# Sigmoids ahead of the gating steps, more buffers and one shift for four tiles, in the first stage of a triangle kernel

## The chip, the cores and the metric

The kernel runs on one core of a Trainium2 chip. The metric is the time of one execution on the device, in microseconds (us). The program is one launch; all five engines (TensorE, VectorE, ScalarE, GpSimd, SyncE) and the DMA work in it side by side. In the profile PE is TensorE's matmuls, PEld its weight loads, DVE is VectorE, ACT is ScalarE, POOL is GpSimd and SP is SyncE, which here only issues transfers.

## The reference

Two layers on `x` of 384 x 384 positions with 128 channels, all in float32. The first is a triangle product, the second a gated row operation. Cut to what matters:

```python
def layer0(x, ...):
    z = layernorm(x)                                   # over the channels
    left = (z @ Wl + bl) * sigmoid(z @ Wlg + blg)
    right = (z @ Wr + br) * sigmoid(z @ Wrg + brg)
    core = einsum('bikh,bjkh->bijh', left, right)
    zo = layernorm(core) @ Wout + bout
    return x + sigmoid(x @ Wg + bg) * zo

def layer1(pair, ...):
    left = pair @ (W_left + W_eq) + b_left + b_eq
    right_sum = sum(pair @ W_right + b_right, axis=2)
    out = left * right_sum * sigmoid(pair @ W_gate + b_gate)
    return layernorm(out @ W_out + b_out + pair)
```

## The kernel before

It has three stages. The first makes `left` and `right` of all positions and writes them to the scratch tensor `lr_d`; it also writes the transposed, normalized input to `xt_d` for the third. The second makes `core`, one channel `h` at a time. The third does the rest. The change lies in the first and at the seam to the second.

The first stage works in chunks of eight rows `i` by 128 positions `k` (144 chunks), each in two steps of four tiles of 128 positions by 128 channels: 288 steps. Sixteen steps fill one `lr` tile of 64 rows (a block; there are 18), which is then stored in eight slices. Pools and the parts of a step (line numbers as the profile has them, cuts marked with `...`):

```python
inp = ctx2.enter_context(tc.tile_pool(name="p2in", bufs=3))           # lrh, second stage
...
with tc.tile_pool(name="p1x", bufs=6, side="right") as xp, \
     tc.tile_pool(name="p1w", bufs=2, side="right") as wp, \
     tc.tile_pool(name="p1s", bufs=5, side="right") as sp, \
     tc.tile_pool(name="p1z", bufs=4, side="right") as ztp, \
     ...
     tc.tile_pool(name="p1t", bufs=2, space=PSUM) as tps, \
     tc.tile_pool(name="p1p", bufs=3, space=PSUM) as pps:

    def stats(n, q, half):                    # L223, L225, VectorE: two bn_stats, two bn_aggr
        ...
    def powers(n, q):                         # L236 to L239, GpSimd: rs, and nd = mean - std of eight tiles
        ...
    def shift(n, q):                          # L248, GpSimd
        kb, ig, c = chunks[n]
        z = wp.tile([P, 4, C], F32, tag="z", name="z")
        for r in range(4):
            rr = 4 * q + r
            nd = nds[kb, ig][:, c * XR + rr:c * XR + rr + 1]
            seq(nc.gpsimd.tensor_scalar(z[:, r, :], loaded[n][:, rr, :], nd, None, ALU.subtract))
        return z

    def front(n, q, z):                       # L255 TensorE, L257 ScalarE
        pt = tps.tile([P, 4, P], F32, tag="pt", name="pt")
        for r in range(4):
            seq(nc.tensor.transpose(pt[:, r, :], z[:, r, :], ident))
        zt = zts[n, q] = ztp.tile([P, 4, P], F32, tag="zt", name="zt")
        seq(nc.scalar.copy(zt, pt))

    def store_zt(n, q):                       # L262, SP
        ...
        seq(nc.sync.dma_start(out=xt_d[:, i0:i0 + 4, kb, :], in_=zts.pop((n, q))))

    def store_slice():                        # L276, SP: one eighth of a full lr tile to lr_d
        ...

    def back(n, q, half):                     # L291 TensorE, L298 ScalarE, L299 VectorE
        ...
        t = lr[kb, ig]
        pr = pps.tile([P, 2, 4 * H], F32, tag="pr", name="pr")
        for r in range(2):
            seq(nc.tensor.matmul(pr[:, r, :], lhsT=zts[n, q][:, 2 * half + r, :], rhs=wz, start=True, stop=True))
        sg = wp.tile([P, 2, 2 * H], F32, tag="sg", name="sg")
        for r in range(2):
            rr = 4 * q + 2 * half + r
            rs = normed[n][2][:, rr:rr + 1]
            seq(nc.scalar.activation(sg[:, r], pr[:, r, 2 * H:], AF.Sigmoid, scale=rs))
            seq(nc.vector.scalar_tensor_tensor(
                t[:, :, c * XR + rr, :],
                pr[:, r, :2 * H].rearrange("k (h s) -> k h s", s=2),
                rs,
                sg[:, r].rearrange("k (h s) -> k h s", s=2),
                ALU.mult, ALU.mult,
            ))
        ...

    for k, (n, q) in enumerate(steps):
        if k + 2 < len(steps):
            zs[k + 2] = shift(*steps[k + 2])
        if k + AHEAD - 1 < len(steps):        # AHEAD = 6
            powers(*steps[k + AHEAD - 1])
        for half in range(2):
            back(n, q, half)
            if half == 0 and k + 1 < len(steps):
                front(*steps[k + 1], zs.pop(k + 1))
            if k + AHEAD < len(steps):
                stats(*steps[k + AHEAD], half)
        if q == NQ - 1:
            del loaded[n], normed[n]
            load_chunk(n + 6)                 # L114, SP
            if chunks[n][2] == G // XR - 1:
                store_nd(*chunks[n][:2])      # a small transpose and store at the end of a block
        store_zt(n, q)
        store_slice()
        ...
        if k == 20:
            late_weights()                    # L197 to L212: weights of the later stages
        if k == len(steps) - 2 * G // 4 + 16:
            for h in range(3):
                load_h(h)                     # L92, L93, SP: lrh tiles of the first three channels
```

So one step on TensorE is two matmuls of 128x512, four transposes for the next step, and two matmuls more; in float32 each matmul shows in the profile as two records. Pools hand out their tiles in turn: a tile can be written again when its last reader is done, be it an engine or a transfer. The scheduler keeps each engine's instructions in program order. In the second stage, nine matmuls a channel read an `lrh` tile and an `rr` tile filled from it; when a channel is done, the tile of the channel three later is loaded.

Of the kernel before, what the change touches and what calls it, by code (L numbers as in the profile page):

```python
# [8 lines left out]
F32 = mybir.dt.float32  # L9
AF = mybir.ActivationFunctionType  # L10
ALU = mybir.AluOpType
# [3 lines left out]
P = 128  # L15
# [4 lines left out]
def triangle_then_gated_row_kernel(ctx: ExitStack, tc: tile.TileContext, a: dict, out: bass.AP):  # L20
# [12 lines left out]
    nc = tc.nc  # L33
    x = a["x"].rearrange("b i j c -> (b i) j c")
    y = out.rearrange("b i j c -> (b i) j c")
    N, _, C = x.shape
    H = a["L0_conv_Wl"].shape[1]
    assert C == P and H == P and N % P == 0
    NB = N // P
    G = 64  # L40
    NG = N // G
    XR = 8
# [13 lines left out]
    def seq(ins):  # L56

        return tc.keep_in_program_order(ins)
# [20 lines left out]
    end2 = ctx.enter_context(ExitStack())  # L79
    with ExitStack() as ctx2:  # L80
        lrp = ctx2.enter_context(tc.tile_pool(name="lr", bufs=2))
        inp = ctx2.enter_context(tc.tile_pool(name="p2in", bufs=3))
        loaded2 = {}

        def load_h(h):

            if h < H:
                t = inp.tile([P, NB, N, 2], F32, tag="lrh", name="lrh")
                src = lr_d[h].rearrange("(b p) i s -> p b (i s)", p=P)
                i1 = 2 * G * (NG - KEEP)  # L90
                dst = t.rearrange("p b i s -> p b (i s)")
                seq(nc.sync.dma_start(out=dst[:, :NB - 1], in_=src[:, :NB - 1]))  # L92
                seq(nc.sync.dma_start(out=dst[:, NB - 1, :i1], in_=src[:, NB - 1, :i1]))  # L93
                loaded2[h] = t

        with tc.tile_pool(name="p1x", bufs=6, side="right") as xp, \
             tc.tile_pool(name="p1w", bufs=2, side="right") as wp, \
             tc.tile_pool(name="p1s", bufs=5, side="right") as sp, \
             tc.tile_pool(name="p1z", bufs=4, side="right") as ztp, \
             tc.tile_pool(name="p1d", bufs=2, side="right") as dp, \  # L100
             tc.tile_pool(name="p1t", bufs=2, space=PSUM) as tps, \
             tc.tile_pool(name="p1p", bufs=3, space=PSUM) as pps:
# [3 lines left out]
            loaded, normed = {}, {}  # L106
# [83 lines left out]
            def late_weights():  # L190

                ps = tps.tile([P, 4, P], F32, tag="pt", name="pw")
                m2 = wp.tile([P, 4, C], F32, tag="z", name="m2")[:, 0]
                seq(nc.vector.tensor_scalar(m2, avg, go, -1.0, ALU.mult, ALU.mult))
                seq(nc.tensor.matmul(ps[:, 0], lhsT=m2, rhs=wout0, start=True, stop=True))  # L197
                seq(nc.vector.scalar_tensor_tensor(wc, wout0, go, ps[:, 0], ALU.mult, ALU.add))
                seq(nc.tensor.matmul(ps[:, 1, 0:1], lhsT=wout0, rhs=bo, start=True, stop=True))
                seq(nc.vector.tensor_add(bz, ps[:, 1, 0:1], bout0))  # L200

                seq(nc.vector.tensor_add(wleft, wleft, weq))
                seq(nc.vector.tensor_add(bleft, bleft, beq))
                for n, (w, b) in enumerate(((wleft, bleft), (wgate, bgate), (wright, bright))):
                    p4 = ps[:, 2, n:n + 1]
                    seq(nc.tensor.matmul(p4, lhsT=w, rhs=bout1, start=True, stop=True))
                    seq(nc.vector.tensor_sub(b, b, p4))
                seq(nc.vector.tensor_scalar(bright, bright, float(N), None, ALU.mult))  # L210

                seq(nc.vector.tensor_scalar(lns, lns, -1.0, None, ALU.mult))  # L212
# [14 lines left out]
            def powers(n, q):  # L227


                if q == NQ - 1:  # L230
                    _, mv, rs, sd = normed[n]
                    kb, ig, c = chunks[n]
                    if c == 0:
                        nds[kb, ig] = dp.tile([P, G], F32, tag="nd", name="nd")
                    nd = nds[kb, ig][:, c * XR:(c + 1) * XR]
                    seq(nc.gpsimd.tensor_scalar(sd, mv[:, :, 1], EPS, 1.0, ALU.add, ALU.mult))  # L236
                    seq(nc.gpsimd.tensor_tensor(rs, sd, mhalf[:, :XR], ALU.pow))
                    seq(nc.gpsimd.tensor_tensor(sd, sd, rs, ALU.mult))
                    seq(nc.gpsimd.tensor_tensor(nd, mv[:, :, 0], sd, ALU.subtract))  # L239

            def shift(n, q):

                kb, ig, c = chunks[n]
                z = wp.tile([P, 4, C], F32, tag="z", name="z")
                for r in range(4):
                    rr = 4 * q + r
                    nd = nds[kb, ig][:, c * XR + rr:c * XR + rr + 1]
                    seq(nc.gpsimd.tensor_scalar(z[:, r, :], loaded[n][:, rr, :], nd, None, ALU.subtract))  # L248
                return z

            def front(n, q, z):
# [6 lines that stand above are left out]
# [24 lines left out]
            def back(n, q, half):  # L282


                kb, ig, c = chunks[n]
                if c == 0 and q == 0 and half == 0:
                    lr[kb, ig] = lrp.tile([P, H, G, 2], F32, tag="lr", name="lr")
# [3 lines that stand above are left out]
                    seq(nc.tensor.matmul(  # L291
                        pr[:, r, :], lhsT=zts[n, q][:, 2 * half + r, :], rhs=wz, start=True, stop=True
                    ))
                sg = wp.tile([P, 2, 2 * H], F32, tag="sg", name="sg")
                for r in range(2):
                    rr = 4 * q + 2 * half + r
                    rs = normed[n][2][:, rr:rr + 1]
                    seq(nc.scalar.activation(sg[:, r], pr[:, r, 2 * H:], AF.Sigmoid, scale=rs))  # L298
                    seq(nc.vector.scalar_tensor_tensor(  # L299
                        t[:, :, c * XR + rr, :],  # L300
                        pr[:, r, :2 * H].rearrange("k (h s) -> k h s", s=2),
                        rs,
                        sg[:, r].rearrange("k (h s) -> k h s", s=2),
                        ALU.mult, ALU.mult,
                    ))
                if c == G // XR - 1 and q == NQ - 1 and half == 1:
                    if (kb, ig) in kept:
                        kept[kb, ig] = t
                    else:
                        full.extend((kb, ig, hs, t) for hs in range(0, H, HS))  # L310
# [3 lines left out]
            nds, zts = {}, {}  # L314
# [12 lines left out]
# [3 lines that stand above are left out]
                if k + AHEAD - 1 < len(steps):  # L330
# [9 lines that stand above are left out]
                    load_chunk(n + 6)  # L340
                    if chunks[n][2] == G // XR - 1:
                        store_nd(*chunks[n][:2])
                store_zt(n, q)
                store_slice()
                if k == 4:
                    for t, src in later:
                        load(t, src)
                if k == 20:
                    late_weights()
                if k == len(steps) - 2 * G // 4 + 16:  # L350
                    assert not full
                    for h in range(3):
                        load_h(h)


        rrp, spool, rp = (end2.enter_context(tc.tile_pool(name=n, bufs=b, side="right", reuse_waits="tile"))
                     for n, b in (("p2r", 2), ("stats", 1), ("rstd", 2)))
        with tc.tile_pool(name="p2out", bufs=2, side="right", reuse_waits="tile") as op, \
             tc.tile_pool(name="p2sq", bufs=1, side="right", reuse_waits="tile") as qp, \
             tc.tile_pool(name="p2ps", bufs=2, space=PSUM, reuse_waits="tile") as ps:  # L360
            csum = spool.tile([P, NB, N], F32, name="csum")
# [1 line left out]
            seq(nc.vector.memset(csum, 0.0))  # L363
            seq(nc.vector.memset(csq, 0.0))

            right = {}

            def fill(h):
# [13 lines left out]
            for h in range(H):  # L382
                fill(h + 1)
                t, rr = loaded2.pop(h), right.pop(h)
# [23 lines left out]
    with ExitStack() as ctx3:  # L408
# [3 lines left out]
        xp, fp, inp, op = pool("p3x", 7), pool("p3f", A + 4), pool("p3in", 3), pool("p3out", 3)  # L412
        wp, sp, late = pool("p3w", 4), pool("p3s", 4), []
# [275 lines left out]
```

## Time and profile before

| | |
|---|---|
| time, median of 3 (lowest, highest) | 3457.69 us (3457.24, 3458.84) |
| span of the profiled execution | 3460.0 us |
| TensorE matmuls busy | 3363.2 us, 97% |
| VectorE, ScalarE, GpSimd busy | 2528.3, 2014.3, 2627.0 us |
| first stage, first projection to first matmul of the second | 15.4 to 1273.2 us |
| second stage | 1273.2 to 2016.0 us |
| third stage | 2016.0 to 3460.0 us |
| DMA, first stage | 229 GB/s |
| `zt` store: issue to landing, median | 5.4 us |
| `lr_d` slice store, chunk load | 7.1, 6.8 us |

The profile is one execution on the chip. A group is all instructions of one line, engine and operation; its row gives the tile written and those read, shapes, count, busy time, mean duration in ns, and then the idle time of that engine just before them with what ended most of it. A timeline row has start, length, engine, line, operation and count, and in brackets the idle time before and who ended it. The ends of matmuls are modelled, since they are pipelined: a busy TensorE need not be at its full pace, and the starts of records tell more than their lengths. Idle time of an engine that isn't on the path that sets the end costs nothing.

### The profile page before, as it was taken

How to read it: one execution, taken by the hardware profiler on the slowest of the kernel's cores; microseconds unless marked ns; L12 is line 12 of the kernel's file. 1: busy time of each engine (PE TensorE's matmuls, PEld its weight loads, DVE VectorE, ACT ScalarE, POOL GpSimd, SP SyncE). 2: the span in 40 equal slices, each digit the busy share in tenths (PEclk: the TensorE clock that was granted, in tenths of full speed). 3: DMA queues.
4: the chain of work that ended last, by engine and by line, in shares of the span. 5: the costliest groups of instructions: out<-in, count | busy, mean ns of one | idle time of the engine just before them, and what ended most of it. 6: DMA issues, size and time to landing. Idle time of an engine off the chain costs nothing.

```text
span 3460.0 us, 48243 instructions
## 1 busy us (share of the span) xinstructions
PE 3363.2 (97%) x12584; PEld 1986.6 (57%) x12584; DVE 2528.3 (73%) x8074; ACT 2014.3 (58%) x4049; POOL 2627.0 (76%) x4131
## 2 busy tenths in 40 slices
PE   8999999999999999999999989999999999999997
PEld 3444444444444446666666656777777777777775
DVE  6676677667766755555555568888888888888887
ACT  4555555555555543333333356777777777777776
POOL 7788788778877865656555538888888888888887
PEclk9999999999999999999999999999999999999999
DMA  5888778887888749999999987888888999888883
GB/s 141 231 256 257 224 227 255 250 241 220 255 252 245 215 150 282 281 282 285 281 284 282 282 285 230 265 272 272 273 271 272 273 274 274 271 271 270 271 269 101
DMA packets 924616, 872.90 MB, mean 252 GB/s; under 512 B 24868, under 2 KB 839720, under 8 KB 924344
## 3 DMA queue, kind: packets, MB, share of 16 engines
q1 hardware_dynamic: 904960, 794.32, 73.6%
q0 software_dynamic: 13152, 71.37, 10.1%
q10 hardware_dynamic: 6232, 4.13, 0.4%
q8 instruction: 103, 1.69, 0.2%
q14 instruction: 169, 1.38, 0.1%
HBM read 507.85 MB, written 361.89 MB: 251 GB/s over the span
## 4 chain that ended last, share of the span: by engine, by line
PE 85%; DMA 6%; ACT 3%; DVE 3%; POOL 1%; issue 1%; ACTq 0%; POOLq 0%; SPq 0%; DVEq 0%
PE pr L291 23%; PE pc L388 21%; PE pr L526 7%; PE py L555 7%; PE pg L489 7%; PE pl L544 7%; PE pg L543 7%; DMA xt_d<-zt 5%; PE py L556 3%; PE pt L255 3%; DVE lr L299 2%; ACT sg L298 1%; ACT zt L257 1%; ACT py L586 1%; DVE st L223 1%
## 5 line engine op out<-in xcount | busy, mean ns | idle before, releaser
L291 PE MATMUL pr<-wz,zt 128*128 128x512 f32 x2304 | 1120.3, 611 | 48.7 <-ACT zt L257 44.5
L298 ACT ACTIVATE sg<-pr,rs 128x256 f32<-128x256 f32 x1152 | 546.7, 475 | 534.0 <-DVE lr L299 326.7
L299 DVE SCALAR_TENSOR_TENSOR lr<-pr,rs,sg 128x256 f32<-128x256 f32 x1152 | 550.8, 478 | 376.2 <-ACT sg L298 368.5
L388 PE MATMUL pc<-rr,lrh 128*128 128x384 f32 x2304 | 743.3, 486 | 2.3 <-DVE lr L299 2.3
L291 PEld LDWEIGHTS pr<-wz,zt 128*128 128x128 f32 x2304 | 395.5, 191 | 554.6 <-issue 281.3
L248 POOL TENSOR_SCALAR z<-xt,nd 128x128 f32<-128x128 f32 x1152 | 675.4, 606 | 31.5 <-issue 22.0
L388 PEld LDWEIGHTS pc<-rr,lrh 128*128 128x128 f32 x2304 | 451.8, 196 | 293.7 <-issue 2.8
L586 ACT ACTIVATE py<-py,nm,rs 128x128 f32<-128x128 f32 x1152 | 495.5, 430 | 185.3 <-POOL rs L579 92.6
L555 PEld LDWEIGHTS py<-wo,u 128*128 128x128 f32 x2304 | 377.5, 191 | 102.4 <-ACT wo L537 1.7
L397 DVE TENSOR_TENSOR csum<-csum,ct 128x1152 f32<-128x1152 f32 x128 | 178.9, 1398 | 344.8 <-ACT ct L394 344.8
L374 POOL COPY rr<-lrh 128x768 f32<-128x768 f32 x128 | 184.7, 1443 | 306.2 <-DMA lrh<-lr_d 299.7
L517 POOL TENSOR_TENSOR cs<-ct,rt 128x384 f32<-128x384 f32 x384 | 406.7, 1063 | 3.2 <-PE pr L526 2.6
L598 POOL TENSOR_TENSOR yt<-yt,lnb 128x384 f32<-128x384 f32 x384 | 406.3, 1058 | 2.9 <-DVE yt L597 2.6
L394 ACT COPY ct<-pc 128x1152 f32<-128x1152 f32 x128 | 143.2, 1119 | 450.0 <-PE pc L388 446.4
L555 PE MATMUL py<-wo,u 128*128 128x128 f32 x2304 | 403.0, 275 | 1.2 <-ACT wo L537 1.2
L570 DVE BATCH_NORM_STATS2 st<-py 128x6 f32<-128x128 f32 x1152 | 266.4, 287 | 94.6 <-PE py L556 93.8
L526 PE MATMUL pr<-cs,wc 128*128 128x384 f32 x768 | 319.4, 498 | 4.5 <-POOL cs L517 4.4
L556 PE MATMUL py<-ident,x1T 128*128 128x128 f32 x1152 | 314.0, 273 | 0.0
L544 PE MATMUL pl<-x1T,mat_L_conv_W_left 128*128 128x384 f32 x768 | 312.1, 488 | 1.5 <-ACT gT L491 1.5
L543 PE MATMUL pg<-x1T,mat_L_conv_W_gate 128*128 128x384 f32 x768 | 312.1, 488 | 0.9 <-ACT gT L491 0.5
L489 PE MATMUL pg<-xt,mat_L_conv_Wg 128*128 128x384 f32 x720 | 292.0, 487 | 0.0
L546 ACT ACTIVATE g<-pg,col_L_conv_b_gate 128x384 f32<-128x384 f32 x384 | 223.1, 581 | 99.1 <-PE pg L543 94.0
(96 smaller groups left out, 4727.3 us busy)
## 6 DMA issues: line engine op xcount, KB each, us to landing
lr_d<-lr SPq DMA_DIRECT2D x128, 1024.0 KB, 7.1
lrh<-lr_d SPq DMA_DIRECT2D x128, 768.0 KB, 7.8
xt_d<-zt SPq DMA_DIRECT2D x288, 256.0 KB, 5.4
ct<-core_d SPq DMA_DIRECT2D x96, 768.0 KB, 6.4
rt<-rstd_d SPq DMA_DIRECT2D x96, 768.0 KB, 8.0
out_dram<-yt SPq DMA_DIRECT2D x95, 768.0 KB, 4.9
core_d<-ct SPq DMA_DIRECT2D x125, 576.0 KB, 8.7
xt<-in_x_dram SPq DMA_DIRECT2D x140, 512.0 KB, 6.8
```

What stands on the lines that cost most here:

```text
L248: seq(nc.gpsimd.tensor_scalar(z[:, r, :], loaded[n][:, rr, :], nd, None, ALU.subtract))
L291: seq(nc.tensor.matmul(pr[:, r, :], lhsT=zts[n, q][:, 2 * half + r, :], rhs=wz, start=True, stop=True))
L298: seq(nc.scalar.activation(sg[:, r], pr[:, r, 2 * H:], AF.Sigmoid, scale=rs))
L299: seq(nc.vector.scalar_tensor_tensor(t[:, :, c * XR + rr, :], pr[:, r, :2 * H].rearrange("k (h s) -> k h s", s=2), rs, sg[:, r].rearrange( ...
L388: seq(nc.tensor.matmul(pc[:, ib, :N], lhsT=t[:, kb, ib * P:(ib + 1) * P, 0], rhs=rr[:, kb], start=(kb == 0), stop=(kb == NB - 1),))
L489: seq(nc.tensor.matmul(pg[:, :N], lhsT=wg0, rhs=r["xT"], start=True, stop=True))
L526: seq(nc.tensor.matmul(pr[:, :N], lhsT=wc, rhs=r["cs"], start=True, stop=True))
L543: seq(nc.tensor.matmul(pg2[:, :N], lhsT=wgate, rhs=r["x1T"], start=True, stop=True))
L544: seq(nc.tensor.matmul(pl[:, :N], lhsT=wleft, rhs=r["x1T"], start=True, stop=True))
L555: seq(nc.tensor.matmul(py[:, s], lhsT=r["u"][:, s], rhs=r["wo"], start=True, stop=False))
L556: seq(nc.tensor.matmul(py[:, s], lhsT=r["x1T"][:, s], rhs=ident, start=False, stop=True, is_transpose=True))
L586: seq(nc.scalar.activation(py[:, s], py[:, s], AF.Identity, bias=nm[:, n, b:b + 1], scale=rs[:, n, b:b + 1]))
```

## The change

It does four things in the first stage. A pair's two sigmoids are given one after the other, ahead of the pair's two gating steps, and each has a tile of its own (six such tiles in turn, in place of two tiles with room for a pair). The transposed tiles `zt` get six buffers in place of four. The shift of the four tiles of a step is one GpSimd operation with the column of `nd` broadcast along the channels, in place of four operations with a scalar column each. To make room, only two `lrh` tiles of the second stage are there during the first; the third is in a pool of its own, opened when the first stage's tiles are given back, and is loaded from then on. Its aim is that ScalarE and VectorE wait less for each other, that the evacuation of transposes waits less for stores, and that GpSimd has fewer instructions. The diff, cut to its core:

```diff
-        inp = ctx2.enter_context(tc.tile_pool(name="p2in", bufs=3))
+        inp = [ctx2.enter_context(tc.tile_pool(name="p2in", bufs=2))]
...
-                t = inp.tile([P, NB, N, 2], F32, tag="lrh", name="lrh")
+                t = inp[h % 3 // 2].tile([P, NB, N, 2], F32, tag="lrh", name="lrh")
...
-             tc.tile_pool(name="p1w", bufs=2, side="right") as wp, \
+             tc.tile_pool(name="p1w", bufs=6, side="right") as wp, \
              tc.tile_pool(name="p1s", bufs=5, side="right") as sp, \
-             tc.tile_pool(name="p1z", bufs=4, side="right") as ztp, \
+             tc.tile_pool(name="p1z", bufs=6, side="right") as ztp, \
...
-                z = wp.tile([P, 4, C], F32, tag="z", name="z")
-                for r in range(4):
-                    rr = 4 * q + r
-                    nd = nds[kb, ig][:, c * XR + rr:c * XR + rr + 1]
-                    seq(nc.gpsimd.tensor_scalar(z[:, r, :], loaded[n][:, rr, :], nd, None, ALU.subtract))
+                z = wp.tile([P, 4, C], F32, tag="z", name="z", bufs=2)
+                nd = nds[kb, ig][:, c * XR + 4 * q:c * XR + 4 * q + 4]
+                seq(nc.gpsimd.tensor_tensor(
+                    z, loaded[n][:, 4 * q:4 * q + 4, :], nd.unsqueeze(2).to_broadcast([P, 4, C]), ALU.subtract
+                ))
...
-                sg = wp.tile([P, 2, 2 * H], F32, tag="sg", name="sg")
+                r0 = 4 * q + 2 * half
+                rs = [normed[n][2][:, r:r + 1] for r in range(r0, r0 + 2)]
+                sg = [wp.tile([P, 2 * H], F32, tag="sg", name="sg") for _ in range(2)]
                 for r in range(2):
-                    rr = 4 * q + 2 * half + r
-                    rs = normed[n][2][:, rr:rr + 1]
-                    seq(nc.scalar.activation(sg[:, r], pr[:, r, 2 * H:], AF.Sigmoid, scale=rs))
+                    seq(nc.scalar.activation(sg[r], pr[:, r, 2 * H:], AF.Sigmoid, scale=rs[r]))
+                for r in range(2):
                     seq(nc.vector.scalar_tensor_tensor(
-                        t[:, :, c * XR + rr, :],
+                        t[:, :, c * XR + r0 + r, :],
                         pr[:, r, :2 * H].rearrange("k (h s) -> k h s", s=2),
-                        rs,
-                        sg[:, r].rearrange("k (h s) -> k h s", s=2),
+                        rs[r],
+                        sg[r].rearrange("k (h s) -> k h s", s=2),
                         ALU.mult, ALU.mult,
                     ))
...
-                    for h in range(3):
+                    for h in range(2):
                         load_h(h)
...
+        with tc.tile_pool(name="p2more", bufs=1, side="right", reuse_waits="tile") as more, \
...
+            inp.append(more)
+            load_h(2)
             right = {}
```

More of the change, by code (lines that the diff above doesn't have):

```diff
@@ L194, in late_weights @@
                 ps = tps.tile([P, 4, P], F32, tag="pt", name="pw")
-                m2 = wp.tile([P, 4, C], F32, tag="z", name="m2")[:, 0]
+                m2 = wp.tile([P, 4, C], F32, tag="z", name="m2", bufs=2)[:, 0]
                 seq(nc.vector.tensor_scalar(m2, avg, go, -1.0, ALU.mult, ALU.mult))
@@ L357, in triangle_then_gated_row_kernel @@
                      for n, b in (("p2r", 2), ("stats", 1), ("rstd", 2)))
-        with tc.tile_pool(name="p2out", bufs=2, side="right", reuse_waits="tile") as op, \
+        with tc.tile_pool(name="p2more", bufs=1, side="right", reuse_waits="tile") as more, \
+             tc.tile_pool(name="p2out", bufs=2, side="right", reuse_waits="tile") as op, \
              tc.tile_pool(name="p2sq", bufs=1, side="right", reuse_waits="tile") as qp, \
```

## The prediction

> **What bounds the kernel now.** I read the page from its stages to its waits, then the trace step by step. The change touches the first stage (lines 223 to 299, slices 1 to 15 of the page's 40) and the first loads of the second. The busy times by stretch put a number on it (columns: stretch, length, busy time and instructions of PE, PEld, DVE, ACT, POOL, granted clock, DMA share, GB/s): from the first projection at 15.4 us to the second stage at 1273.2.
>
> ```profile
> 15.40:1273.20 1257.80, 1203.14 (x3481) 536.08 (x3481) 878.13 (x3438) 685.63 (x1457) 994.27 (x1722) 0.99 0.80 229
> 1273.20:2016.00 742.80, 742.80 (x2304) 451.76 (x2305) 399.47 (x256) 289.86 (x254) 430.93 (x764) 1.00 0.90 279
> ```
>
> TensorE is 95.7% busy in the first stage, with 54.66 us idle. The groups show large mutual waits elsewhere:
>
> ```profile
> L291 PE MATMUL pr<-wz,zt 128*128 128x512 f32 x2304 | 1120.3, 611 | 48.7 <-ACT zt L257 44.5
> L298 ACT ACTIVATE sg<-pr,rs 128x256 f32<-128x256 f32 x1152 | 546.7, 475 | 534.0 <-DVE lr L299 326.7
> L299 DVE SCALAR_TENSOR_TENSOR lr<-pr,rs,sg 128x256 f32<-128x256 f32 x1152 | 550.8, 478 | 376.2 <-ACT sg L298 368.5
> L248 POOL TENSOR_SCALAR z<-xt,nd 128x128 f32<-128x128 f32 x1152 | 675.4, 606 | 31.5 <-issue 22.0
> ```
>
> The second sigmoid of a pair waits for the gating step of the first, since both share a tile. TensorE never waits for a sigmoid by name; it waits for `zt`, the evacuated transposes. The waits from 115 to 1200 us (total us, times, longest) say why `zt` is late:
>
> ```profile
> PE pr L291 <- ACT zt L257: 43.9, 41, 2.7
> ACT zt L257 <- DMA xt_d<-zt: 37.0, 30, 2.6
> ```
>
> One of the four `zt` buffers is still being stored. TensorE's timeline, undisturbed and stalled:
>
> ```profile
> 118.50 0.60 PE L255 MATMUL pt<-ident,z 128*128 128x128 f32 x4
> 118.94 3.90 PE L291 MATMUL pr<-wz,zt 128*128 128x512 f32 x8
> 122.67 0.60 PE L255 MATMUL pt<-ident,z 128*128 128x128 f32 x4
> 123.11 3.84 PE L291 MATMUL pr<-wz,zt 128*128 128x512 f32 x8
> 126.78 0.60 PE L255 MATMUL pt<-ident,z 128*128 128x128 f32 x4
> ...
> 341.18 1.88 PE L291 MATMUL pr<-wz,zt 128*128 128x512 f32 x4
> 345.00 2.43 PE L291 MATMUL pr<-wz,zt 128*128 128x512 f32 x4 [1.95 <-ACT zt L257]
> 347.23 1.06 PE L255 MATMUL pt<-ident,z 128*128 128x128 f32 x4
> 348.08 4.47 PE L291 MATMUL pr<-wz,zt 128*128 128x512 f32 x8
> ```
>
> A step takes 4.11 us (122.67 to 126.78), every second one 4.17. In that there is a wait that the busy column hides, for matmul ends are modelled. The weight loads between show it:
>
> ```profile
> 119.38 0.19 PEld L291 LDWEIGHTS pr<-wz,zt 128*128 128x128 f32 x1 [0.24 <-issue]
> 119.80 0.19 PEld L291 LDWEIGHTS pr<-wz,zt 128*128 128x128 f32 x1 [0.24 <-issue]
> 120.85 0.30 PEld L291 LDWEIGHTS pr<-wz,zt 128*128 128x128 f32 x2 [0.86 <-ACT zt L257]
> ```
>
> Loads follow each other at the pace of the matmuls, 0.42 to 0.43 us. The next was due at 120.23 and came at 120.85, held for `zt`. Eight records at 0.43 and four transposes at 0.11 (0.44 from 118.50 to 118.94) make 3.88; a step of 4.11 holds 0.23 of hidden idle time, one of 4.17 holds 0.29. The second stage has no such gap: 322 ns a record of 384 columns (742.80 / 2304), so 430 for 512.
>
> **What the Trainium skill says.** Perfetto Trace Analysis, Optimization Strategy: a gap that returns on the engine that should be saturated can mean too few buffers for the next tile. The trace agrees: it returns about every 70 us. TensorE: Matmul & The Clock Gate, Part 1: 512 columns take 215.7 ns warm, and the clock is halved after an idle window. A record here, at 430 ns, is two such passes; after the stall at 345 us the granted clock is 0.73 until 348 and 0.79 until 352.4, and transposes take 1.06 in place of 0.60. GPSIMD Engine Reference, 3.1: a two-input operation costs about 2.6 cycles an element; line 517's 128x384 TENSOR_TENSOR takes 1063 ns here, 2.77 ns an element. Its section 8: GpSimd contends with VectorE where that has two SBUF inputs. The gating step reads one input from PSUM, and takes 450 to 488 ns throughout, with GpSimd busy 79% of the stage.
>
> **The change part by part.** In the built program every operation keeps its number and its order on its engine, but for the shift and one load; so work on TensorE stays and only waits can go.
>
> 1. More `zt` buffers, four to six. A block of 16 steps (one `lr` tile) issues 16 `xt_d` stores of 256 KB, eight loads of 512 KB and eight `lr_d` stores of 1024 KB, these in its first eight steps. Those bring 12.6 MB in 8 x 4.14 = 33.1 us; from 160 to 210 us the DMA moved 288 GB/s at a full share, or 9.5 MB. The queue lags by 3.1 MB, 10.6 us. With 5.4 us from issue to landing a buffer is free 16 us after its copy, and four buffers give 16.5: at the edge. Six at 3.9 us a step give 23.4 against a lag of 12.2 (12.6 MB in 31.2 us) + 5.4 = 17.6. Over a block, 16.8 MB take 58 us of 62.5, so it is worked off in time.
> I summed the start-to-start times of all steps less 4.11: 71.6 us, of which 8.7 is the late preparation of weights, 1.1 the first step, 2.5 block boundaries, 4.9 the odd steps, and 54.3 lies in steps 5 to 13 of the blocks: 43.9 idle, about 10 slow clock. I take 90%: 49 us.
> 2. Sigmoids ahead, in their own tiles. In a step at 600 us the sigmoids start at 600.33 and 601.36, then the copy to `zt` at 601.73, 0.37 behind the second; it ends at 602.31 and the weight load comes at 602.36, though it was due at 601.80 and, with 0.15 of load, needed by about 602.1. Without the wait for the gating step the second sigmoid starts at about 600.8 (0.47 after the first), the copy at 601.2, done at 601.8. So it moves ahead by some 0.5 us, more than the 0.3 it lacks. The hidden wait is 288 x 0.23 + 4.9 = 71 us; I take 85%: 60. At the end of the stage the chain shortens by 0.5.
> In the built program the first gating step waits for both sigmoids. VectorE has per half step two gating steps, two statistics and two aggregates, about 1.46 us (2.93 a step: 210 us in the 300 from 300 us on) of 1.94, so it fits.
> 3. One shift for four tiles: 512 x 2.77 = 1.42 us for 4 x 0.606 = 2.42. GpSimd saves 288 us busy; TensorE's idle time names it nowhere: 0.
> 4. The room: the third `lrh` tile loads only when the stage ends. 1 MB at 288 GB/s is 3.6, plus some 2: at about 6 us into the second stage, when its fill also starts now (1279.36). Cost 1 us.
>
> Sum: 49 + 60 + 0.5 - 1 = 108.5; 3457.7 - 108.5 = 3349.
>
> **The rivals.** (a) The hidden wait doesn't go, because the 2.05 us chain of two sigmoids and two gating steps sets the pace in another way (the `pr` banks come free no sooner). For it: 2 x 2.05 is 4.10, nearly the step. Against it: TensorE's late load names `zt`, and three `pr` tiles leave 5.8 us. It gives 3408. (b) The wait moves on to the `xt` loads behind the `lr_d` stores, or the DMA becomes the bound: at 3.88 a step it is busy 58 of 62.5 us. Against it: a load is issued about six steps (23 us) before its statistics, with lag and landing of 19. If the DMA only gives 270 GB/s, blocks take 65: 18 x 2.5 = 45 us back, 3394. (c) The third `lrh` load is late and the second stage at 279 GB/s doesn't make it up: 5 to 10 us, 3357.
>
> **Range and chances.** With every stall and hidden wait gone: 3457.7 - 54.3 - 71 = 3332. With (b) in part, about 3385. Range 3332 to 3388. Faster by over 2% means below 3388.5: 0.85. Within 2%, where (a) or (b) hold: 0.13. Slower needs a new bound that nothing here shows: 0.02.
>
> **What would show it.** Right: TensorE's wait for `zt` near zero, steps near 3.9 us, weight loads 0.43 apart across the groups, a first stage of about 1150 us, the shift at 1.3 to 1.5 us. Wrong: steps still at 4.1 (a); VectorE's statistics or `zt` waiting for the DMA (b); TensorE gaps within 20 us of the second stage's start (c); a shift above 3 us, with which GpSimd exceeds the step.

## The result and the profile after

The changed kernel takes 3333.57 us (median of 4 runs, 3333.14 to 3333.74) against 3458.27 for the kernel before on the same chip: a ratio of 0.9637, with a 95% interval of 0.962 to 0.9654. That is 124.7 us less, where 108.5 had been predicted.

The stretches of the changed kernel, with the columns of the prediction's first fence:

```profile
15.30:1145.70 1130.40, 1124.45 (x3480) 554.50 (x3480) 852.10 (x3438) 621.63 (x1457) 613.70 (x863) 1.00 0.88 253
1145.70:1888.50 742.80, 742.76 (x2303) 451.98 (x2304) 401.28 (x256) 289.78 (x254) 438.79 (x764) 1.00 0.90 281
1888.50:3331.80 1443.30, 1410.68 (x6794) 996.25 (x6792) 1243.57 (x4343) 1035.76 (x2335) 1192.77 (x1629) 0.99 0.86 260
```

All of the gain lies in the first stage, 1130.40 us for 1257.80. The second stage takes 742.80 us as before, and the third 1443.3 for 1444.0. TensorE's busy time in the first stage also fell, from 1203.14 to 1124.45 us, although it does the same matmuls: part of what had counted as busy was waiting or a lower clock. Its groups on the page after, with those of ScalarE, VectorE and GpSimd:

```profile
L291 PE MATMUL pr<-wz,zt 128*128 128x512 f32 x2304 | 1042.8, 594 | 0.7 <-ACT zt L257 0.7
L298 ACT ACTIVATE sg<-pr,rs 128x256 f32<-128x256 f32 x1152 | 482.8, 470 | 507.8 <-PE pr L291 375.1
L300 DVE SCALAR_TENSOR_TENSOR lr<-pr,rs,sg 128x256 f32<-128x256 f32 x1152 | 504.8, 480 | 274.8 <-ACT sg L298 226.9
L246 POOL TENSOR_TENSOR z<-xt,nd 128x512 f32<-128x512 f32 x288 | 299.8, 1041 | 43.4 <-POOL z L246 30.0
```

TensorE's idle time before line 291 is 0.7 us where it was 48.7, and the sigmoids now wait mostly for TensorE and no longer for the gating steps. They are just as idle as before (507.8 us for 534.0); only the cause has changed. Two steps of TensorE's timeline, and the weight loads at the change of group:

```profile
117.69 0.60 PE L255 MATMUL pt<-ident,z 128*128 128x128 f32 x4
118.13 3.60 PE L291 MATMUL pr<-wz,zt 128*128 128x512 f32 x8
121.56 0.60 PE L255 MATMUL pt<-ident,z 128*128 128x128 f32 x4
122.00 3.60 PE L291 MATMUL pr<-wz,zt 128*128 128x512 f32 x8
125.44 0.60 PE L255 MATMUL pt<-ident,z 128*128 128x128 f32 x4
```

```profile
118.56 0.19 PEld L291 LDWEIGHTS pr<-wz,zt 128*128 128x128 f32 x1 [0.24 <-issue]
118.99 0.19 PEld L291 LDWEIGHTS pr<-wz,zt 128*128 128x128 f32 x1 [0.24 <-issue]
119.42 0.19 PEld L291 LDWEIGHTS pr<-wz,zt 128*128 128x128 f32 x1 [0.24 <-ACT zt L257]
119.85 0.19 PEld L291 LDWEIGHTS pr<-wz,zt 128*128 128x128 f32 x1 [0.24 <-issue]
```

A step takes 3.87 us (117.69 to 121.56), against the 3.88 that the prediction worked out from the distances between records. The load that needs `zt` comes 0.43 us behind the one before, like every other: 0.24 is the usual distance between the end of one load and the next, so the label "ACT zt" there is no loss any more. Of the 287 step-to-step times, 267 lie at 3.87 or 3.88, 17 at 3.98 or 3.99 (the extra transpose at the end of a block), and only three are longer: the first two steps, and the late preparation of weights with 12.45.

### The profile page after: what moved, and what is told of

Its sections match the earlier page's. It is cut to its first block, busy times and chain, and to the rows that moved or that the text cites. A ratio compares the mean times of both kernels' runs of the same rounds, so it can differ in the third digit from the quotient of the medians.

```text
span 3331.8 us, 48534 instructions
## 1 busy us (share of the span) xinstructions
PE 3283.0 (99%) x12584; PEld 2004.5 (60%) x12584; DVE 2503.8 (75%) x8074; ACT 1949.2 (59%) x4049; POOL 2250.2 (68%) x3267
## 4 chain that ended last, share of the span: by engine, by line
PE 62%; ACT 1%; POOL 1%; DVE 0%; issue 0%; DMA 0%; POOLq 0%; SPq 0%; ACTq 0%
PE pc L392 22%; PE pr L530 7%; PE py L559 7%; PE pg L493 7%; PE pl L548 7%; PE pg L547 7%; PE py L560 4%; ACT py L590 1%; POOL rs L579 0%; PE pq L514 0%; DMA xt<-nd_d 0%; POOL yt L602 0%; PE pxt L506 0%; DVE yt L601 0%; DVE st L574 0%
## 5 line engine op out<-in xcount | busy, mean ns | idle before, releaser
L291 PE MATMUL pr<-wz,zt 128*128 128x512 f32 x2304 | 1042.8, 594 | 0.7 <-ACT zt L257 0.7
L298 ACT ACTIVATE sg<-pr,rs 128x256 f32<-128x256 f32 x1152 | 482.8, 470 | 507.8 <-PE pr L291 375.1
L300 DVE SCALAR_TENSOR_TENSOR lr<-pr,rs,sg 128x256 f32<-128x256 f32 x1152 | 504.8, 480 | 274.8 <-ACT sg L298 226.9
L291 PEld LDWEIGHTS pr<-wz,zt 128*128 128x128 f32 x2304 | 415.3, 191 | 412.5 <-issue 346.9
L246 POOL TENSOR_TENSOR z<-xt,nd 128x512 f32<-128x512 f32 x288 | 299.8, 1041 | 43.4 <-POOL z L246 30.0
L236 POOL TENSOR_SCALAR sd<-mv 128x8 f32<-128x8 f32 x144 | 28.4, 197 | 436.5 <-DVE mv L225 436.4
```

Source lines behind the costliest of these rows:

```text
L298: seq(nc.scalar.activation(sg[r], pr[:, r, 2 * H:], AF.Sigmoid, scale=rs[r]))
L300: seq(nc.vector.scalar_tensor_tensor(t[:, :, c * XR + r0 + r, :], pr[:, r, :2 * H].rearrange("k (h s) -> k h s", s=2), rs[r], sg[r].rearra ...
```

## The experiments

My theory was that two losses were separate, stalls for `zt` buffers and a hidden wait in every step, and that the second came from the `sg` tile that a pair of sigmoids shared. Rivals were a bound in the DMA, another limit on TensorE's pace, and another cause for the sigmoids' order. The kernel before was timed beside each set of runs, with medians of 3458 to 3466 us.

**Only the buffers.** The old `back` and `shift` in the changed kernel; six `zt` buffers and the seam stay:

```diff
-                sg = [wp.tile([P, 2 * H], F32, tag="sg", name="sg") for _ in range(2)]
+                sg = wp.tile([P, 2, 2 * H], F32, tag="sg", name="sg", bufs=2)
 # sigmoid and gating step in turn in one loop over r; four tensor_scalar operations in shift
```

> Only the six zt buffers (with the seam that makes room for them); sigmoids and shift as before. If the stalls and the hidden wait are two separate losses, the stalls go (54 us) and steps stay at 4.11 and 4.17 us: 3404 us, no idle of TensorE before line 291 by name. If the DMA were the true bound, buffers only postpone: 3445 or more. If the even pace of 4.11 were TensorE's own, this alone would be the whole gain of the change: 3334.

3410.26 us (3409.68 to 3411.27), ratio 0.9857 (0.984 to 0.9875). The waits of this kernel from 115 to 1130 us, then a weight load from its trace:

```profile
ACT sg L298 <- DVE lr L299: 276.7, 489, 0.9
PE pr L291 <- ACT zt L257: 1.1, 4, 0.3
```

```profile
601.89 0.19 PEld L291 LDWEIGHTS pr<-wz,zt 128*128 128x128 f32 x1 [0.24 <-issue]
602.93 0.30 PEld L291 LDWEIGHTS pr<-wz,zt 128*128 128x128 f32 x2 [0.85 <-ACT zt L257]
```

TensorE's named wait for `zt` is gone, 1.1 us for 43.9, and no `zt` copy waits for a store. The hidden one is there as before: 1.04 us between two loads in place of 0.43. The DMA was not the bound, and 4.11 us was not TensorE's own pace. Buffers alone are worth 48.5 us.

**Only the sigmoids.** The changed kernel with four `zt` buffers and the old shift:

```diff
-             tc.tile_pool(name="p1z", bufs=6, side="right") as ztp, \
+             tc.tile_pool(name="p1z", bufs=4, side="right") as ztp, \
```

> Only the sigmoids ahead in own tiles; four zt buffers and the old shift. If the losses simply add, the hidden wait goes (71 us): 3387. If the faster step meets the DMA's lag, as the arithmetic of buffers says (four buffers give 4 x 3.88 = 15.5 us against 17.6 of lag and landing), the stalls grow to about 100 us: some 3430, with steps of 3.88 outside the bursts and a longer wait of zt for its store.

3422.30 us (3418.98 to 3431.41), ratio 0.9896 (0.9873 to 0.9919). Its waits:

```profile
ACT zt L257 <- DMA xt_d<-zt: 82.0, 60, 3.3
PE pr L291 <- ACT zt L257: 55.0, 36, 2.7
```

Outside the bursts (the steps in which a finished block is being stored) steps are 3.87 us, and inside them `zt` waits for its store 82.0 us where it waited 37.0: half of what the sigmoids bring is lost again. Alone, the two parts bring 48.5 and 36.4 us; in one kernel they bring 125.

**The changed kernel with four buffers**, the same edit with the new shift:

> The changed kernel with four zt buffers. By the arithmetic of the lag (15.5 us given, 17.6 needed in a burst) stalls of about 5 us a block: 3334 + 16 x 5 to 6, about 3420 to 3430, like the sigmoids alone. If faster sigmoids had also freed zt earlier, so that four suffice: below 3350.

3424.22 us (3423.02 to 3427.68), ratio 0.9883 (0.9868 to 0.9898). At the faster step, two more buffers are worth 90.6 us (3424.2 less 3333.6; 91.6 against the next run, which was timed beside this one), not the 48.5 of the slower one.

**The old shift** in the changed kernel:

```diff
-                seq(nc.gpsimd.tensor_tensor(
-                    z, loaded[n][:, 4 * q:4 * q + 4, :], nd.unsqueeze(2).to_broadcast([P, 4, C]), ALU.subtract
-                ))
+                for r in range(4):  # four tensor_scalar operations, as before
```

> The changed kernel with the old shift of four operations. GpSimd is then busy 8 x 0.59 + 2.3 = 7.0 us of the 7.75 of two steps. If the shift lies off the path, as predicted: 3334. If at the faster step GpSimd comes near the bound and transposes wait for it: 3345 to 3370, with TensorE idle before line 255.

3332.58 us (3331.74 to 3334.18), ratio 0.9617 (0.9603 to 0.9632), with the same steps of 3.87: the shift is worth nothing. Weight loads of the transposes wait 37.4 us for it by name, but no more than 0.3 at a time, and TensorE doesn't stand still.

**Which tile carries the wait.** First, own `sg` tiles but the old order in the program; second, the new order but one `sg` tile for a pair:

```diff
 # old order, own tiles
-                for r in range(2):
-                    seq(nc.scalar.activation(sg[r], ...))
-                for r in range(2):
-                    seq(nc.vector.scalar_tensor_tensor(...))
+                for r in range(2):
+                    seq(nc.scalar.activation(sg[r], ...))
+                    seq(nc.vector.scalar_tensor_tensor(...))
```

```diff
 # new order, one tile
-                sg = [wp.tile([P, 2 * H], F32, tag="sg", name="sg") for _ in range(2)]
+                sg = wp.tile([P, 2, 2 * H], F32, tag="sg", name="sg", bufs=3)
                 ...
-                    seq(nc.scalar.activation(sg[r], ...))
+                    seq(nc.scalar.activation(sg[:, r], ...))
```

> The changed kernel with the old order in the program (sigmoid, gating step, sigmoid, gating step), but each sigmoid in a tile of its own. If the shared sg tile made the second sigmoid wait, as the prediction has it: 3334, steps 3.88. If it is the order of the program, in which both engines read the same pr tile: the wait stays, steps 4.1, about 3404.

> The changed kernel with the sigmoids ahead, but both of a pair in one tile (three such tiles). If the shared sg tile is the cause: the wait stays, 3404. If the order is: 3334, steps 3.88.

Old order with own tiles: 3410.85 us (3410.22 to 3412.05). New order with one tile: 3333.61 us (3332.28 to 3334.64). The shared `sg` tile, which the prediction named, plays no part. In the first of the two the wait stands unchanged:

```profile
ACT sg L298 <- DVE lr L299: 276.6, 489, 0.9
PE pr L291 <- ACT zt L257: 1.1, 4, 0.3
```

What is left as the tie between the second sigmoid and the first gating step is `pr`, one tile for a pair in PSUM, where the results of matmuls lie. It spans two banks, one for each matmul of the pair, and both engines read it. So, in the old order and with own `sg` tiles, a `pr` tile of one bank for each matmul:

```diff
-             tc.tile_pool(name="p1p", bufs=3, space=PSUM) as pps:
+             tc.tile_pool(name="p1p", bufs=6, space=PSUM) as pps:
-                pr = pps.tile([P, 2, 4 * H], F32, tag="pr", name="pr")
+                pr = [pps.tile([P, 4 * H], F32, tag="pr", name="pr") for _ in range(2)]
```

> The old order in the program (sigmoid, gating step, sigmoid, gating step), sigmoids in own tiles, and the matmul results too in a tile of one PSUM bank each (six in place of three of two banks). If the shared pr tile is what carries the wait: no wait of the second sigmoid for the first gating step, 3334, steps 3.88. If only the order counts, whatever the tiles: 3404.

3332.41 us (3331.25 to 3332.59), ratio 0.9617 (0.96 to 0.9633). Its sigmoids on the page:

```profile
L298 ACT ACTIVATE sg<-pr,rs 128x256 f32<-128x256 f32 x1152 | 545.3, 473 | 421.9 <-PE pr L291 421.9
```

None of their idle time is put down to a gating step. Both engines only read `pr`, and these two operations read different banks of it; the wait was put in by the program's dependence on the tile, not by the data. Turning the order, as the change does, and splitting the tile are two ways to be rid of it.

**Five buffers.** The changed kernel with `bufs=5` for `zt`:

> The changed kernel with five zt buffers. The lag arithmetic of the prediction (12.2 us of lag + 5.4 to land = 17.6 us) against 5 x 3.88 = 19.4 us leaves 1.8 us: 3334 to 3350. If six are needed in full, as a lag at 280 GB/s would have it, about 2 us a block: 3360 to 3370.

3358.04 us (3355.83 to 3360.05), ratio 0.9706 (0.9689 to 0.9722): 24.5 us more than six, although the arithmetic left 1.8 us to spare. In its trace 15 steps, one to a block, are late by 1.6 us on average. SP's own queue shows what it had left out. Around the end of a block, with five buffers:

```profile
209.68 0.45 SPq L114 DMA_DIRECT2D xt<-in_x_dram  x1
218.78 0.45 SPq L270 DMA_DIRECT2D nd_d<-ndt  x1
219.28 0.58 SPq L262 DMA_DIRECT2D xt_d<-zt  x1
219.95 0.46 SPq L276 DMA_DIRECT2D lr_d<-lr  x1
```

For 9.1 us SP issues nothing: the small `nd` store waits for its copy, and the `zt` store behind it waits along. So, still with five buffers, I put each `zt` store ahead of the chunk load and the `nd` store:

```diff
+                store_zt(n, q)
                 if q == NQ - 1:
                     ...
-                store_zt(n, q)
                 store_slice()
```

> Five zt buffers, and in the transfer queue each store of zt ahead of the chunk load and of the small nd store at the end of a chunk or block, for which SP waits. Five buffers cost 24 us more than six, though the arithmetic left 1.8 us to spare. If the stores are late because they stand in the queue behind something that waits: 3334 to 3342. If the lag of the DMA itself is longer than worked out: 3352 or more, as with five buffers before (3358).

3333.95 us (3331.95 to 3333.97), ratio 0.9632 (0.9614 to 0.9649). With this order five buffers are as good as six. SP's waits for the `nd` store from 115 to 1130 us (total us, times, longest), before the turn and after it:

```profile
SPq L270 <- ACT ndt L269: 135.7, 16, 8.6
SPq L270 <- ACT ndt L269: 74.2, 16, 4.7
```

No `zt` copy waits for a store any more. The lateness was in the queue's order, not in a lag of the DMA beyond the estimate.

**The late weights in parts.** Most of what is left above 3.87 us a step is the preparation of later weights, 8.6 us. Cut in three, after steps 20, 22 and 25, the matmuls of a part first and then the column work; `m2` gets a tile of its own:

```diff
-                if k == 20:
-                    late_weights()
+                if k in (20, 22, 25):
+                    late_weights((20, 22, 25).index(k))
```

> The changed kernel with the late weights prepared in three parts, after steps 20, 22 and 25, each with its matmuls first and the column work after them, and a tile of their own for the first product. In the changed kernel this place costs TensorE 12.45 - 3.87 = 8.6 us in one step. If the waits there are those between TensorE and VectorE in turn, and of the shift for its tile: 3326. If the steps are stretched elsewhere instead: 3334.

3326.36 us (3324.56 to 3327.29), ratio 0.9598 (0.9584 to 0.9613), 7.2 us below the changed kernel; the summed steps of the two traces differ by as much, 1124.45 less 1117.14. TensorE at this place in the changed kernel, then in this one:

```profile
97.94 1.88 PE L291 MATMUL pr<-wz,zt 128*128 128x512 f32 x4
102.49 0.46 PE L197 MATMUL pw<-mat_L_conv_Wout,m 128*128 128x128 f32 x2 [2.67 <-issue]
103.39 0.58 PE L199 MATMUL pw<-col_L_conv_onorm_b,mat_L_conv_Wout 128*128 128x1 f32 x2 [0.44 <-DVE wc L198]
```

```profile
106.12 1.88 PE L289 MATMUL pr<-wz,zt 128*128 128x512 f32 x4
107.84 0.38 PE L200 MATMUL pw<-mat_L_conv_Wout,m 128*128 128x128 f32 x2
108.06 0.28 PE L201 MATMUL pw<-col_L_conv_onorm_b,mat_L_conv_Wout 128*128 128x1 f32 x2
108.20 1.96 PE L289 MATMUL pr<-wz,zt 128*128 128x512 f32 x4
```

The small matmuls now stand between two groups without a gap.

**Parts and own PSUM tiles together:**

> Weights in three parts together with PSUM tiles of one bank in the old order: the waits of both runs gone, and the last gating steps of the stage not behind both sigmoids. 3325, the same as the parts alone within 2 us, since the gain of own PSUM tiles is the one that the new order has already.

3324.89 us (3324.22 to 3326.52), ratio 0.9612 (0.9598 to 0.9627). It is faster than the kernel before and than the changed kernel, but can't be told from the parts alone, as expected.

**A full operand for the shift.** Here the shift subtracts the chunk's other four tiles, and so leaves out the mean; only durations are read from it:

```diff
-                    z, loaded[n][:, 4 * q:4 * q + 4, :], nd.unsqueeze(2).to_broadcast([P, 4, C]), ALU.subtract
+                    z, loaded[n][:, 4 * q:4 * q + 4, :], loaded[n][:, 4 - 4 * q:8 - 4 * q, :], ALU.subtract
```

> The changed kernel with a full 128x512 tile as the second operand of the shift in place of the broadcast column; it subtracts the chunk's other four tiles and so leaves out the shift by the mean. If the broadcast operand is what makes the shift cheaper than 2.77 ns an element (1041 ns measured for 512): about 1420 ns. If two SBUF inputs of VectorE slow the third stage's operations instead: 1041 ns again. Time 3334 either way, since the shift lies off the path.

3332.8 us (one run). The operation's row:

```profile
L246 POOL TENSOR_TENSOR z<-xt 128x512 f32<-128x512 f32 x288 | 362.1, 1276 | 12.0 <-PE pt L255 9.4 <-PE pw L197 2.1
```

1276 ns, where the broadcast column takes 1041: neither of the two expected numbers. The broadcast explains 235 ns of the error, and the estimate the rest.

## Why the prediction was right, and where it was not

The time, 3333.6, lies inside the range of 3332 to 3388, at its low end: both losses were there and both went, and the discount on the second was too careful. That it comes so close to the prediction's floor of 3332 is partly luck: the buffers brought 5.8 us less than the 54.3 of stalls, and the sigmoids 5.7 more than the 71 of hidden wait.

1. *Buffers, 49 us.* Alone they brought 48.5; the summed steps fell from 1251.19 us to 1200.82, by 50.4 of the 54.3 put down to stalls. The lag arithmetic had the order of size, but not the queue: it took each store as issued when its data were there. (Its lag for the faster step also comes to 12.5 us and not to 12.2: 12.6 MB at 288 GB/s take 43.7 us, less 31.2.) Five buffers showed the difference, and the turned order showed its cause.
2. *Sigmoids, 60 us.* This is the mis-sized term. With the buffers there, they brought 76.7 (3410.3 less 3333.6), for 71 of hidden wait found in the trace and 85% of it taken. The summed steps say the same: 1200.82 us with buffers alone and 1124.45 after, 76.4 less. The reading of weight loads was right, and no discount was due: in the changed kernel the copy to `zt` ends 0.21 us before its weight load in the median, where a load that was held for it had followed it by 0.05. The step's cause was named wrongly: not the shared `sg` tile but the shared `pr` tile, read in turn in the program's order.
3. *Shift, 0.* Right, by the run with the old shift. Its duration was put at 1.42 us and is 1.04: the mean of line 517 was taken as a price per element, without a fixed part, and the broadcast was not counted.
4. *Room, 1 us.* TensorE waits 1.9 us at the seam where it waited 2.3, and nowhere after it in the second stage: 0.

With the measured sizes the sum is 48.5 + 76.7 = 125.2 for 124.7. Rival (a), a chain that sets the pace in another way, fell with steps of 3.87 us. Rival (b), the DMA, did not come: from 157 to 202 us it moved 304 GB/s at a full share while TensorE stayed busy all 45 us, more than the 288 assumed. But with four buffers it took back about half of what the sigmoids bring, 40 of 77 us. The 45 us that the prediction gave this rival don't follow from its own figures: at 270 GB/s the 16.8 MB of a block take 62 us, not 65, and 62.5 were there. Rival (c) did not come.

## What to carry to other kernels

When ends of matmuls are modelled, read the starts of records and weight loads: a load that comes later than the pitch of its neighbours is idle time of TensorE that no busy column shows. Two engines that only read one tile can still be made to wait for each other by the tile's bookkeeping; give the readers' instructions in an order that needs no wait, or a tile each. (The two engines read different banks here; no run shows them reading one bank at once.) A faster step needs more buffers for the same transfer queue, so try such parts together before judging one; and let no store stand in the queue behind one whose data come later.

## What the runs showed of the hardware

TensorE's clock in the kernel before shows why its stalls differed in cost. The lowered clock comes in stretches whose starts (346.40, 418.08 and 626.30 us, among others) lie whole multiples of 3.413 us apart. Two pauses on this grid, a slot with the pause and the slot after it (the granted clock is the third number from the end):

```profile
203.04:206.46 3.42, 1.71 (x4) 0.41 (x3) 1.72 (x8) 0.63 (x2) 2.95 (x6) 1.00 1.03 305
206.46:209.87 3.41, 2.41 (x9) 1.41 (x10) 1.51 (x6) 1.77 (x4) 1.66 (x3) 1.00 1.06 304
342.99:346.40 3.41, 1.46 (x5) 0.68 (x5) 1.18 (x7) 1.44 (x3) 3.25 (x7) 1.00 1.13 335
346.40:349.82 3.42, 3.42 (x9) 1.76 (x8) 2.32 (x9) 1.42 (x3) 1.58 (x4) 0.50 1.07 315
```

The pause of 1.95 us before 345.00 falls into one slot, in which TensorE is busy for 1.46 us of 3.41, and the next slot ran at 0.50. The pause of 2.70 us before 207.46 is longer, but 206.46 divides it between two slots, busy for 1.71 and 2.41 us, and the clock stayed. From 110 to 1200 us of this trace, the six slots in which TensorE was busy for 43% or less were each followed by a slot at half clock, and none of the others, at 46% or more, was. So the "idle window" of the prediction need not be idle throughout, and where a pause lies counts as well as its length. This is read from one trace's records; no run was made to test it.

GpSimd's TENSOR_TENSOR with full operands takes 996 ns in the median for 384 elements and 1277 for 512, which as two points of a line give 2.2 ns an element and about 155 fixed. The split is rough: the 384-element operations run in the third stage, and their mean is 1059. The Trainium skill's page GPSIMD Engine Reference, section 3.1, has about 2.6 cycles an element, by estimate 2.17 ns at the 1.2 GHz which the page gives, and so agrees with the slope; the prediction's 2.77 had the fixed part in it. With a column broadcast along the row, 512 take 1041.
